# Layer 0 of a convolution stack: two-patch expansion rows first, then single-patch rows; convolution steps taken in pairs

## The chip, the core and the metric

The kernel runs on one core of a Trainium2 chip. The metric is the device time of one launch in microseconds, lower being better; the comparison uses medians of several launches of both kernels on the same chip.

## What is computed

The input `x` has four images of 64 channels, 256 x 256 pixels, in f32. Four layers follow, each of the form `x = x + layer(group_norm(x))`. The change touches the first layer alone, whose core in the reference is

```python
x = jnp.einsum('bchw,oc->bohw', x, w_in)            # 64 -> 384 channels
# per 8x8 patch: rfft2, times fft_filter, irfft2
x = lax.conv_general_dilated(x, w_dw, (1, 1), [(1, 1), (1, 1)], feature_group_count=C)   # 3x3 per channel
x1, x2 = jnp.split(x, 2, axis=1)
x = jax.nn.gelu(x1, approximate=False) * x2          # 192 channels
return jnp.einsum('bchw,oc->bohw', x, w_out)         # 192 -> 64 channels
```

Per channel, the patch filter and the 3 x 3 convolution are one linear map: the 64 outputs of an 8 x 8 patch depend on the 64 pixels of the patch itself and on those of its neighbours (right, below, diagonal, as the patches are cut here).

## The kernel before

Each image is an array of 32 x 32 patches. A **block** `p` is a strip of NR = 11 rows of patches in an image, and there are three to an image, so 12 blocks. A block is worked in four quarters `kb`, each of 48 hidden channels with their gate partners. A quarter has two stages:

1. **Expansion**, `expand(p, kb, t)`, for up to 12 rows `t` of patches. The normalized input `xn` of the row stands still in TensorE, and the weights `win` stream past. Even rows take two patches at a time (`pairs`, line 444: 32 instructions on tiles of 64 x 128), odd rows one patch at a time (line 450: 64 instructions on tiles of 64 x 64). The result lies in PSUM (`psu`) and is copied to the SBUF tile `u` by ScalarE (ACT) and VectorE (DVE), half a row each: four copies on each engine for a row of pairs (line 459), three for a row of singles (lines 461 to 463). Of the 12 blocks four have 12 rows and eight have 11, because a strip at the edge of the image lacks one.
2. **Convolution**, `convolve(p, kb, g)`, for 12 steps `g`. Each step first makes the patches' **own** products (line 494, tiles of 64 x 64, 16 instructions), then the **neighbours'** products, added to the same PSUM (line 503, 48 instructions, 64 rows by up to 28 columns). Then ACT applies GELU (line 510, twice) and DVE multiplies by the gate (line 511, twice); the result `h` is sent to DRAM by a DMA that GpSimd (POOL) issues (line 514).

Around the steps of block `p` stands other work, put there by hand:

- `unit()` runs one sixteenth of the last projection of block `p - 1`: `project` makes its products (lines 591 and 598) in a PSUM tile `po`, and DVE adds them to the residual `r` (line 607, or lines 610 and 612 and the statistics of line 618). `load_half` then issues the loads for a later unit on the queue of SyncE (SP).
- `load_w` loads weights of the convolution; `load_next` loads what the next block or image needs: in the first three quarters four-row pieces `st` of the next image, whose statistics `next_stats` takes on DVE (line 320, two instructions a piece), in the last quarter rows `x` of the next block, which `normalize_x` turns into `xn` on ACT (line 256). `next_norms` advances a waiting group norm by one of its parts.

The order on TensorE, DVE, ACT and SP is the order in which the program is written. PSUM is handed out by `banks` in strict rotation over four tiles of two banks: `tag=f"p{next(turn) % 4}"`. A row of expansion takes two of the four, a convolution step two, a unit one, so each use waits until the tile's previous content, four hand-outs back, has been copied or multiplied away.

The order of a quarter before:

```python
if t == NR - 2: load_w(...)
if t >= NR - 1: load_next(kb)
...
if g % 3 == 0: unit()
convolve(p, kb, g)
if g < 2: load_next(kb)
if g in (1, 2, 4, 5) and loaded: next_stats(b + 1, loaded.pop(0))
```

Of the kernel before, what the change touches and what calls it, by code (L numbers as in the profile page):

```python
# [18 lines left out]
HID = 192  # L19
# [102 lines left out]
class _Net:  # L122
# [152 lines left out]
    def _layer0(self, ctx, dst):  # L275
# [5 lines left out]
        def banks(name):  # L281

            return pp.tile([128, 2, 512], F32, tag=f"p{next(turn) % 4}", name=name)
# [11 lines left out]
        NR = 11  # L295
        L = CW * NR
        NG = PB // 4
# [134 lines left out]
        def expand(p, kb, t):  # L432

            b, i0 = blocks[p]
            ps = [banks(f"psu_{p}_{kb}_{t}_{s}") for s in range(2)]
            xn = xns[b, i0 + t]
            lo, hi = halves
            pairs = t % 2 == 0
            for k in range(2):
                for m in range(4):  # L440
                    n, at = 2 * (4 * k + m), slice(2 * PB * m, 2 * PB * (m + 1))
                    for s in range(2):
                        if pairs:
                            nc.tensor.matmul(  # L444
                                ps[s][:, k, at], xn[halves[s], n : n + 2].rearrange("p n r w -> p (n r w)"),
                                win[halves[s], kb, 0 : 2 * PB], start=True, stop=True,
                            )
                            continue
                        for odd in range(2):
                            nc.tensor.matmul(  # L450
                                ps[s][halves[1 - odd], k, at], xn[halves[s], n + odd].rearrange("p r w -> p (r w)"),
                                win[halves[s], kb, PB * (1 - odd) : PB * (3 - odd)], start=True, stop=True,
                            )
            at = lambda h, o: u[h, :, t * CW + o : t * CW + o + 8].rearrange("p c (s m) -> p c s m", s=2)
            for s, copy in enumerate((nc.scalar.copy, nc.vector.tensor_copy)):
                v = ps[s][:, :, 0 : 8 * PB].rearrange("p s (m c) -> p c s m", m=4)
                if pairs:
                    for h, o, k, c in ((lo, O1, lo, 0), (hi, O2, lo, PB), (lo, E1 + 1, hi, 0), (hi, E2 + 1, hi, PB)):
                        copy(at(h, 8 * s + o), v[k, c : c + PB])  # L459
                    continue  # L460
                copy(at(slice(0, 128), 8 * s + 1), v[:, 0:PB])
                copy(at(hi, 8 * s + E2 + 1), v[lo, PB:])
                copy(at(lo, 8 * s + O1), v[hi, PB:])  # L463
# [18 lines left out]
                tensor=v.tensor, offset=v.offset + down * CW + o, ap=[v.ap[0], [CW, NR], [step, 2], [1, HC]]  # L482
            )

        def convolve(p, kb, g):

            ps = [banks(f"pc_{p}_{kb}_{g}_{k}") for k in range(2)]
            G = NG * kb + g
            w = wl[p * (HID // 8) + G // 2]
            out = lambda lo, m, k, h: ps[k][lo : lo + m, h, 0:L].rearrange("p (i x j) -> p i x j", i=NR, x=2)  # L490
            for k in range(2):
                for c in range(2):
                    for h in range(2):
                        nc.tensor.matmul(  # L494
                            out(C * c, C, k, h), w[halves[h], k, 2 * (G % 2) + c, 0:C], cells(h, 4 * g + 2 * k + c, 0, 0),
                            start=True, stop=False, tile_position=(h * C, c * C), skip_group_check=True,
                        )
            for n, (c0, m, down, right) in enumerate(UNITS):
                for k in range(2):
                    for c in range(2):  # L500
                        q = C * c + Q * (1 - k)
                        for h in range(2):
                            nc.tensor.matmul(  # L503
                                out(q, m, k, h), w[halves[h], k, 2 * (G % 2) + c, c0 : c0 + m],
                                cells(h, 4 * g + 2 * k + c, down, right),
                                start=False, stop=(n == 2), tile_position=(h * C, q), skip_group_check=True,
                            )
            h = p_h.tile([128, 2, L], F32, tag="h", name=f"h_{p}_{kb}_{g}")
            for k in range(2):
                nc.scalar.activation(h[:, k], ps[k][:, 0, 0:L], AF.Gelu)  # L510
                nc.vector.tensor_mul(h[:, k], h[:, k], ps[k][:, 1, 0:L])  # L511
            if p not in gs:
                gs[p] = p_g.tile([2, HID // 2, 2 * Q, L], F32, tag="g", name=f"g_{p}")
            nc.gpsimd.dma_start(gs[p][:, 2 * G : 2 * G + 2].rearrange("k c p l -> (c p) k l"), h)  # L514

# [125 lines left out]
        with ordered:  # L641
# [44 lines left out]
            lo, hi = halves  # L686
# [6 lines left out]
            for p in range(NB + 1):  # L693
                units = iter([(r, half) for r in range(P) for half in range(2)] if p > 0 else [])
                ahead, first = 1, []
                if p == NB:
                    ctx_u.close()
                    sources.append([pool("l0g1e", 6), pool("l0g6e", 6), pool("l0re", 3)])
                    ahead = 3
                for r in range(ahead):  # L700
                    for half in range(2):
                        first.append((p - 1, r, half))
                        if p == NB:
                            load_half(*first.pop())

                def unit():
                    at = next(units, None)
                    if at:
                        project(p - 1, *at)
                        load_half(p - 1, at[0] + ahead, at[1])  # L710

                if p == NB:
                    for k in range(2 * P):
                        unit()
                    while self.norms:
                        self.next_norms()
                    break
                b, i0 = blocks[p]
                rows = rows_of(p)
                after = rows_of(p + 1) if p + 1 < NB else []  # L720
                fresh = [row for row in after if row not in xns]
                for t in (0, NR):
                    if not 0 <= i0 + t < NP:
                        nc.gpsimd.memset(rows_u[:, :, t], 0.0)
                nk = [] if b + 1 >= B else list(range(p % NI * NJ // NI, (p % NI + 1) * NJ // NI))
                loaded, begun = [], iter(fresh[:4])

                def load_next(kb):
                    if kb == 3:
                        row = next(begun, None)  # L730
                        if row:
                            load_x(row)
                    elif nk:
                        loaded.append(nk.pop(0))
                        load_stats(b + 1, loaded[-1])

                for kb in range(4):
                    for t in range(NR + 1):
                        if 0 <= i0 + t < NP:
                            expand(p, kb, t)  # L740
                        if t in (5, 8) and first:
                            load_half(*first.pop(0))
                        if t == NR - 2:
                            load_w(p * (HID // 8) + NG * kb // 2 + 3)
                        if t >= NR - 1:
                            load_next(kb)
                    for g in range(NG):
                        G = NG * kb + g
                        if g % 2 == 0 and g > 0:
                            load_w(p * (HID // 8) + G // 2 + 3)  # L750
                        if g % 3 == 0:
                            unit()
                        convolve(p, kb, g)
                        if g < 2:
                            load_next(kb)
                        if g < NG - 1:
                            self.next_norms()
                        if kb < 3:
                            if g in (1, 2, 4, 5) and loaded:
                                next_stats(b + 1, loaded.pop(0))  # L760
                        elif 0 <= g - 1 < len(fresh):
                            k = g - 1
                            normalize_x(fresh[k])
                            if k + 4 < len(fresh):
                                load_x(fresh[k + 4])
                for row in rows:
                    if row not in after:
                        xns.pop(row)
# [728 lines left out]
```

## Time and profile before

| | us |
|---|---|
| median of 3 launches (6493.61 to 6522.05) | 6502.17 |
| the profiled execution, own time | 6525.09 |
| its span, first to last instruction | 6523.3 |
| TensorE busy in it | 6001.2 (92%) |
| DVE busy | 4272.8 (66%) |
| ACT busy | 3240.4 (50%) |

The profile page gives, for one execution, the busy time of each engine, the chain of work that ended last, and groups of equal instructions by line with their count, busy time and mean duration, followed by the idle time of the engine just before them and what ended it. The timeline lists instructions in order of time, equal ones merged: start, length, engine, line. "PEld" is the loading of stationary weights in TensorE, shown beside "PE", the products. Layer 0 runs from about 101 us, where the first expansion starts, to about 3960 us.

### The profile page before, as it was taken

The numbers are of one execution on the slowest core, as the hardware profiler recorded it, in microseconds if no ns is written. First come the engines' busy times: TensorE is split into PE (matmuls) and PEld (weight loads), VectorE is DVE, ScalarE is ACT, GpSimd is POOL, SyncE is SP. The second block draws the span as 40 slices with busy tenths as digits, with TensorE's granted clock in tenths as the row PEclk, the third lists the DMA queues.
The fourth block names the chain that finished last, engine by engine and source line by source line (L and its number), as shares of the span: only waits on it lengthen the run. The fifth ranks groups of instructions, "written<-read, shape, count | busy, mean of one in ns | idle before, by whom it ended". The sixth has DMA issues, their size and how long they took to land.

```text
span 6523.3 us, 238228 instructions
## 1 busy us (share of the span) xinstructions
PE 6001.2 (92%) x106712; PEld 3199.7 (49%) x106712; DVE 4272.8 (66%) x5924; ACT 3240.4 (50%) x4564; POOL 1046.6 (16%) x1646
## 2 busy tenths in 40 slices
PE   2999999999999999999999977999899999999988
PEld 1455555555555555555555543333344444443566
DVE  5556665565655565655555546999798889885355
ACT  4344434344443444443444314777787778773211
POOL 3111111111111111111111111111122222221011
PEclk9999999999999999999999978999999999999855
DMA  8487879787888787886868779999576666667899
GB/s 242 136 218 214 230 207 232 218 242 219 245 220 243 219 236 206 229 223 199 228 195 226 207 198 244 226 229 228 148 180 174 170 173 181 170 176 268 325 353 398
DMA packets 878510, 1447.67 MB, mean 222 GB/s; under 512 B 77252, under 2 KB 586452, under 8 KB 875444
## 3 DMA queue, kind: packets, MB, share of 16 engines
q1 hardware_dynamic: 725284, 923.09, 55.9%
q0 software_dynamic: 148672, 500.14, 22.1%
q8 instruction: 843, 13.81, 0.9%
q10 hardware_dynamic: 3536, 9.20, 0.6%
q14 instruction: 175, 1.43, 0.1%
HBM read 932.08 MB, written 500.04 MB: 220 GB/s over the span
## 4 chain that ended last, share of the span: by engine, by line
PE 83%; DMA 7%; ACT 5%; issue 2%; DVE 2%; SPq 1%; POOL 0%; ACTq 0%; DVEq 0%; POOLq 0%
PE pc L503 18%; PE pc L494 12%; PE m L880 10%; PE psu L444 9%; PE one L1121 9%; PE div L1080 7%; ACT u L459 4%; PE psu L450 4%; PE po L591 4%; PE psz L1110 2%; DMA x<-x 2%; PE po L598 2%; DMA g<-g 2%; PE psa L1308 2%; DMA x<-in_x_dram 1%
## 5 line engine op out<-in xcount | busy, mean ns | idle before, releaser
L511 DVE TENSOR_TENSOR h<-h,pc 128x374 f32<-128x374 f32 x1152 | 575.3, 541 | 1216.7 <-ACT h L510 1216.5
L510 ACT ACTIVATE h<-pc 128x374 f32<-128x374 f32 x1152 | 493.1, 480 | 1762.0 <-PE pc L503 1745.9
L503 PE MATMUL pc<-u,w 64*16 64x374 f32 (+2 forms) x27648 | 1241.4, 480 | 3.0 <-issue 3.0
L514 POOL DMA_DIRECT2D g<-h x576 | 414.8, 720 | 2990.7 <-DVE h L511 2800.8
L494 PE MATMUL pc<-u,w 64*64 64x374 f32 x9216 | 881.2, 488 | 6.7 <-DVE u L463 3.9
L503 PEld LDWEIGHTS pc<-u,w 64*16 64x16 f32 (+2 forms) x27648 | 413.3, 92 | 763.5 <-issue 761.6
L444 PE MATMUL psu<-win,xn 64*128 64x96 f32 x8704 | 625.7, 283 | 137.2 <-ACT u L459 124.1
L459 DVE COPY u<-psu 64x384 f32<-64x384 f32 x1088 | 604.3, 555 | 155.1 <-PE psu L444 143.5
L444 PEld LDWEIGHTS psu<-win,xn 64*128 64x128 f32 x8704 | 574.8, 193 | 206.2 <-ACT u L459 159.9
L459 ACT COPY u<-psu 64x384 f32<-64x384 f32 x1088 | 560.5, 515 | 221.1 <-PE psu L444 201.0
L1066 DVE TENSOR_TENSOR q<-xn 128x2313 f32<-128x2313 f32 (+2 forms) x256 | 628.0, 2496 | 1.9 <-ACT xn L256 1.7
L1121 PE MATMUL one<-z,wp 32*32 32x512 f32 x16384 | 598.0, 599 | 19.0 <-issue 14.9
L256 ACT ACTIVATE xn<-x,nb,r 128x1024 f32<-128x1024 f32 (+3 forms) x272 | 486.7, 1792 | 212.4 <-DMA x<-x 140.5
L494 PEld LDWEIGHTS pc<-u,w 64*64 64x64 f32 x9216 | 332.2, 132 | 451.1 <-issue 359.7
L1067 ACT ACTIVATE q<-q 128x2313 f32<-128x2313 f32 (+2 forms) x256 | 529.0, 2087 | 30.8 <-DVE q L1066 29.3
L450 PE MATMUL psu<-win,xn 64*64 64x96 f32 x17408 | 456.5, 253 | 79.3 <-issue 48.6
L1080 PE MATMUL div<-q,ones 64*32 64x512 f32 x8192 | 471.1, 602 | 13.8 <-ACT q L1067 10.9
L1121 PEld LDWEIGHTS one<-z,wp 32*32 32x32 f32 x16384 | 367.2, 103 | 229.7 <-issue 88.3
L450 PEld LDWEIGHTS psu<-win,xn 64*64 64x64 f32 x17408 | 396.8, 138 | 121.4 <-issue 66.7
L1154 POOL DMA_DIRECT2D x<-r x512 | 273.9, 544 | 977.8 <-DVE r L1151 963.9
L591 PE MATMUL po<-g,wo 128*64 128x176 f32 (+1 forms) x3072 | 314.9, 348 | 74.3 <-DMA g<-g 37.9
L880 PE MATMUL m<-t,wk 64*64 64x512 f32 x3072 | 341.1, 588 | 0.0
(162 smaller groups left out, 6672.9 us busy)
## 6 DMA issues: line engine op xcount, KB each, us to landing
g<-h POOLq DMA_DIRECT2D x576, 374.0 KB, 6.4
x<-x SPq DMA_DIRECT2D x240, 640.0 KB, 6.4
w<-wt SPq DMA_DIRECT2D x288, 448.0 KB, 7.0
x<-x SPq DMA_DIRECT2D x100, 1024.0 KB, 14.2
g<-g SPq DMA_DIRECT2D x414, 187.0 KB, 5.0
g<-g SPq DMA_DIRECT2D x736, 93.5 KB, 5.3
x<-in_x_dram SPq DMA_DIRECT2D x256, 256.0 KB, 8.2
x<-o POOLq DMA_DIRECT2D x128, 512.0 KB, 8.2
```

The source lines that it names most:

```text
L444: nc.tensor.matmul(ps[s][:, k, at], xn[halves[s], n : n + 2].rearrange("p n r w -> p (n r w)"), win[halves[s], kb, 0 : 2 * PB], start=True ...
L450: nc.tensor.matmul(ps[s][halves[1 - odd], k, at], xn[halves[s], n + odd].rearrange("p r w -> p (r w)"), win[halves[s], kb, PB * (1 - odd) ...
L459: copy(at(h, 8 * s + o), v[k, c : c + PB])
L494: nc.tensor.matmul(out(C * c, C, k, h), w[halves[h], k, 2 * (G % 2) + c, 0:C], cells(h, 4 * g + 2 * k + c, 0, 0), start=True, stop=False, ...
L503: nc.tensor.matmul(out(q, m, k, h), w[halves[h], k, 2 * (G % 2) + c, c0 : c0 + m], cells(h, 4 * g + 2 * k + c, down, right), start=False, ...
L511: nc.vector.tensor_mul(h[:, k], h[:, k], ps[k][:, 1, 0:L])
L591: nc.tensor.matmul(out(k, s, x), wo1, moving(g1[:, 2 * k], 2 * half + k, s, x), start=(x == 0), stop=False, skip_group_check=True,)
L880: nc.tensor.matmul(rows2(m)[halves[j], s], w[dx][halves[s]], ts[n][halves[s], i, 2 * j : 2 * j + 2, dx : dx + W], start=(dx == 0), stop=(d ...
L1066: nc.vector.tensor_sub(d, p0, p1)
L1067: nc.scalar.activation(d, d, AF.Square)
L1080: ins = nc.tensor.matmul(ps[quarters[j], h], ones[halves[h]], q[n, g, k][halves[h], r + 2 * j : r + 2 * j + 2, o : o + W], start=(m == 0), ...
L1121: ins = nc.tensor.matmul(rows2(ps[g])[quarters[j], k], w[quarters[i]], z[quarters[i], h, 2 * j + dy : 2 * j + dy + 2, dx : dx + W], tile_p ...
```

## The change

The expansion makes the same number of rows of each kind, but in another order: `pairs` holds for `t < 6` instead of even `t`. `convolve` is split at its middle into `own` and `beside`, and the steps are taken two at a time: `own(g)`, `own(g + 1)`, `beside(g)`, `beside(g + 1)`. With it the surrounding work moves: units come before steps 0, 2, 6 and 8 instead of 0, 3, 6 and 9; the weights of the first load and one `load_next` come at the last row of the expansion, and the others before pairs 0, 2 and 4 (in the last quarter two rows at each of two calls); statistics come at the end of each pair while pieces wait; `normalize_x` runs for two rows at the end of a pair; `next_norms` is called after five of six pairs instead of after eleven of twelve steps.

```diff
-            pairs = t % 2 == 0
+            pairs = t < (NR + 1) // 2
...
-        def convolve(p, kb, g):
+        pcs = {}
+        def own(p, kb, g):
-            ps = [banks(f"pc_{p}_{kb}_{g}_{k}") for k in range(2)]
+            ps = pcs[g] = [banks(f"pc_{p}_{kb}_{g}_{k}") for k in range(2)]
...
+        def beside(p, kb, g):
+            ps = pcs.pop(g)
...
                     if kb == 3:
-                        row = next(begun, None)
-                        if row:
+                        for _, row in zip(range(2), begun):
                             load_x(row)
...
-                        if t == NR - 2:
+                        if t == NR:
                             load_w(p * (HID // 8) + NG * kb // 2 + 3)
-                        if t >= NR - 1:
                             load_next(kb)
-                    for g in range(NG):
-                        G = NG * kb + g
-                        if g % 2 == 0 and g > 0:
-                            load_w(p * (HID // 8) + G // 2 + 3)
-                        if g % 3 == 0:
+                    for g in range(0, NG, 2):
+                        if g > 0:
+                            load_w(p * (HID // 8) + (NG * kb + g) // 2 + 3)
+                        if g in (0, 2, 6, 8):
                             unit()
-                        convolve(p, kb, g)
-                        if g < 2:
+                        if g < 6:
                             load_next(kb)
-                        if g < NG - 1:
+                        for k in range(2):
+                            own(p, kb, g + k)
+                        for k in range(2):
+                            beside(p, kb, g + k)
+                        if g < NG - 2:
                             self.next_norms()
                         if kb < 3:
-                            if g in (1, 2, 4, 5) and loaded:
+                            if loaded:
                                 next_stats(b + 1, loaded.pop(0))
-                        elif 0 <= g - 1 < len(fresh):
-                            k = g - 1
+                            continue
+                        for k in range(g, min(g + 2, len(fresh))):
                             normalize_x(fresh[k])
                             if k + 4 < len(fresh):
                                 load_x(fresh[k + 4])
```

More of the change, by code (lines that the diff above doesn't have):

```diff
@@ L497, in convolve @@
                         )
+        def beside(p, kb, g):
+            ps = pcs.pop(g)
+            G = NG * kb + g
+            w = wl[p * (HID // 8) + G // 2]
+            out = lambda lo, m, k, h: ps[k][lo : lo + m, h, 0:L].rearrange("p (i x j) -> p i x j", i=NR, x=2)
             for n, (c0, m, down, right) in enumerate(UNITS):
```

## The prediction

> **What bounds the kernel now.** I read the page's chain first: where does the time that sets the end lie?
>
> ```profile
> PE 83%; DMA 7%; ACT 5%; issue 2%; DVE 2%; SPq 1%; POOL 0%; ACTq 0%; DVEq 0%; POOLq 0%
> PE pc L503 18%; PE pc L494 12%; PE m L880 10%; PE psu L444 9%; PE one L1121 9%; PE div L1080 7%; ACT u L459 4%; PE psu L450 4%; PE po L591 4%; PE psz L1110 2%; DMA x<-x 2%; PE po L598 2%; DMA g<-g 2%; PE psa L1308 2%; DMA x<-in_x_dram 1%
> ```
>
> TensorE carries it. In the convolution (L494, L503) it does so alone; in the expansion (L444, L450) 4% of the span runs through ACT's copies, L459. So the two stages have different limits and I read each from its timeline.
>
> Convolution: the timeline of weight loads through one step and into the next. A group of products starts with its weights, so these starts are a clock (start, length, line).
>
> ```profile
> 1402.91 0.21 PEld L494 LDWEIGHTS pc<-u,w 64*64 64x64 f32 x8 [0.66 <-issue]
> 1403.28 0.16 PEld L494 LDWEIGHTS pc<-u,w 64*64 64x64 f32 x4 [0.16 <-issue]
> 1403.59 0.17 PEld L494 LDWEIGHTS pc<-u,w 64*64 64x64 f32 x4 [0.15 <-issue]
> 1404.36 0.15 PEld L503 LDWEIGHTS pc<-u,w 64*16 64x16 f32 x16 [0.60 <-issue]
> ...
> 1405.65 0.13 PEld L503 LDWEIGHTS pc<-u,w 64*4 64x4 f32 x8 [0.19 <-issue]
> 1406.43 0.21 PEld L494 LDWEIGHTS pc<-u,w 64*64 64x64 f32 x8 [0.65 <-issue]
> ```
>
> Groups inside a half follow each other by 0.31 us. The loads at 1403.59 run one group ahead, so two groups lie between them and the first L503: 0.77 = 0.31 + 0.46. The same at the other end, 1405.65 to 1406.43: 0.31 + 0.47. Each change of half costs 0.15 or 0.16 us, and the first group after it in L494 another 0.06 (0.37, not 0.31). The PE timeline of a step behind a projection shows what a missing change is worth:
>
> ```profile
> 1386.13 0.85 PE L598 MATMUL po<-g,wo 64*64 64x160 f32 x16
> 1386.81 1.46 PE L494 MATMUL pc<-u,w 64*64 64x374 f32 x16
> 1388.20 2.14 PE L503 MATMUL pc<-u,w 64*16 64x374 f32 x48
> 1390.27 1.53 PE L494 MATMUL pc<-u,w 64*64 64x374 f32 x16
> 1391.72 2.14 PE L503 MATMUL pc<-u,w 64*16 64x374 f32 x48
> ```
>
> From start to next start, own products take 1.39 us behind L598, which has the same 64 x 64 tiles, and 1.45 behind neighbours' products; the latter take 2.07.
>
> Expansion: the DVE timeline of alternating rows, then who waited for whom between 432 and 3780 us (total, times, longest).
>
> ```profile
> 1359.62 2.26 DVE L459 COPY u<-psu 64x384 f32<-64x384 f32 x4 [0.45 <-PE psu L444]
> 1361.91 0.56 DVE L461 COPY u<-psu 128x384 f32<-128x384 f32 x1
> 1362.49 0.55 DVE L462 COPY u<-psu 64x384 f32<-64x384 f32 x1
> 1363.05 0.56 DVE L463 COPY u<-psu 64x384 f32<-64x384 f32 x1
> 1364.06 2.26 DVE L459 COPY u<-psu 64x384 f32<-64x384 f32 x4 [0.45 <-PE psu L444]
> ```
>
> ```profile
> PE psu L444 <- ACT u L459: 114.1, 170, 1.6
> ```
>
> DVE works 3.99 of each 4.44 us and then waits 0.45 for TensorE, which itself waits some 0.6 us for PSUM before each row of pairs. Neither engine is full: a slow copy (pairs) must end before a slow product (the next pairs) can start, with only a short single row between.
>
> **What the Trainium skill says.** "TensorEngine Tiling (Array Packing)", Key Properties: changing the tiling mode, not just the tile, drains TensorE. The trace agrees: 0.15 us at 64 x 64 to narrow columns and back, nothing at L598 to L494. The same page, PSUM Bottleneck: packed products may leave the PSUM copies as the limit, to be shared by ScalarE and VectorE. It agrees in the rows: DVE 3.99 of 4.44 us. "TensorE: Matmul & The Clock Gate", What's actually happening: the clock halves after idle windows of some 3.4 us. The stretches of layer 0 show 0.98 to 1.00 granted, so I book no clock gain.
>
> **The change, part by part.**
>
> *Conv pairs.* A quarter (four for each of 12 blocks, so 48) has 12 own-to-neighbour changes; six remain, each 0.15. Changes straight back to own products, without a unit or the expansion between: 11 - 3 = 8 before, 5 - 3 = 2 after; each 0.16 + 0.06. So 6 x 0.15 + 6 x 0.22 = 2.22 us a quarter, x 48 = **-106 us**. The first block has no units, but the same difference: 11 to 5. No instruction is added; own(g + 1) behind own(g) should run at 0.31 a group, as L494 does behind L598.
>
> *Rows.* Six (five) rows of pairs follow each other. DVE needs 2.28 for one (4 x 0.56 and gaps). The loop over two PSUM halves needs, from the copies of a row to those of the row two later, 2.37 (release 1361.69 on PE to copies 1364.06) + 2.26, so 2.31 a row: about equal, DVE nearly full. Single rows: DVE 1.70, loop (1.7 + 1.7)/2, the same. A pair of rows costs 4.02 instead of 4.44. A stage's filling and emptying remain, so some 5.5 such pairs count for 12 rows, 4.5 for 11: 16 x (5.5 + 4.5 + 4.5) x 0.42 = **-97 us**. The end of the copies after TensorE's last row stays as far behind (both orders end in single rows, or the unit covers it).
>
> *New wait, po.* At pair g the rotation gives po the oldest tile, and own(g + 1)'s second half needs it back. Before, a whole step (3.5 us) lay between; now only own(g). With T the end of the previous neighbours' products: the multiplies L511 end at T + 1.63 (1406.43 against 1407.06 + 1.00). If statistics follow (two L320 of 0.68) DVE reaches the additions at T + 3.0 and ends them at T + 4.45 (L607, 1.41 to 1.45) or 4.6 (L610 and L612, 0.8 each). TensorE wants the tile at T + 2.07 (unit) + 1.25 + 0.63 = T + 3.95. So it stalls about 0.5 us, and both neighbours' halves queue behind. Pieces wait at the end of pairs 0, 2, 4, 6 and units stand before 2, 6, 8: three cases in a quarter with four pieces, 7 or 8 a block, 23 an image, three images, less 7 for the block without units: 62 x 0.5 = **+31 us**. Without statistics the additions start when the products are there, T + 2.15, and end by T + 3.8: no stall.
>
> *Loads, norms.* Nothing is added on SP or POOL. load_w moves two rows later, still ahead of its use at step 6 by 20 us against a median landing of 7.0. SP meets load_x for rows 2 and 3 behind the dozen issues of the unit's load_half, some 9 us into the stage, and ACT wants them at about 18: landing takes 8.2 at the median, and ACT already waited 22.4 us for x between 800 and 2000. A late row blocks the GELUs behind normalize_x; TensorE has two to three us of other work. A late st piece blocks DVE at L320 likewise. I take **+10 us**, 0 to 60. POOL's h issues (0.72) come in twos, 2 us apart, with 4 buffers and 14 us to the reuse: no cost; were that cover gone, each GELU would wait for a landing of 6.4. The norm's third part, three times in all, may delay ACT by 2 us: nothing.
>
> Sum: -106 - 97 + 31 + 10 = **-162 us**, against the profiled execution's own 6525.09 (span 6523.3), so 6363 there. That execution lies 23 us above the median of the runs shown, 6502.17; I give the time on the median's scale: 6502 - 162 = **6340 us**.
>
> **Bounds of what the trace doesn't show.** Own behind own: at best no gap (taken), at worst half the change cost stays (+50). Pairs behind pairs: DVE bound alone, 3.98, gives -107; if the loop took 2.45, -60. The po stall: 0 to 1.5 each, 0 to +93.
>
> **The rivals.**
>
> *A, PSUM handed back too late (faster, but less).* In a pair without unit, own(g + 3) starts 1.31 us after the last neighbours' products of g + 1 and needs a tile whose multiply ends 1.18 after them: a margin of 0.1. If ACT or DVE runs 0.4 late, each of the 5 x 48 hand-overs stalls: 96 us, so 6436. For it: the margin. Against: the view shows ACT and DVE idle 2 us and more before each step's GELU.
>
> *B, in-order queues blocked by late loads (slower).* If x and st pieces land more than some 12 us after issue, ACT (last quarter) or DVE (first three) stands, and the GELUs of two steps queue behind instead of one. It decides when each of the 11 blocks that fetch ahead loses over 17.7 us (195/11), giving over 6535; at 22 us, 6580. For: DMA engines are busy 0.83 of the time and will have 5% less. Against: only 22.4 us of such waits in four blocks, mostly beside TensorE's work.
>
> *C, nothing moves.* The changes of half or row might only shift the wait: 6500. The built program does have the new order on TensorE, so no effect would mean that DVE or DMA was the true bound; the idle times above speak against it.
>
> **How the numbers follow.** 0.5% (33 us) is about what a measurement of this kernel can tell from no change. Forecast 0.66, A 0.18 (also faster), B 0.08, C 0.08. Faster 0.84, same 0.08, slower 0.08. The forecast alone spans 6285 (full gains, no stall) to 6400; to leave out no more than 2 in 10 the range takes in A: 6285 to 6445.
>
> **What would show it.** Right: the L444 row's wait for ACT falls from 124 to under 40 us on the page; DVE copies run without the 0.45 gaps; a pair of steps takes 6.7 us, not 7.05; quarters are 49 us or less in the convolution (50.5 to 53 now) and 22 to 24 in the expansion (24 to 27). Stalls of own products on L607 or L612 near 0.5 us, some 62 times, show the new wait. Wrong: gaps between own(g) and own(g + 1) of 0.15, or waits on L511 before every pair, or DMA st and x ending long waits of DVE and ACT.

## The result, and the profile after

The changed kernel takes **6426.33 us** (median of 4, 6421.78 to 6442.22) against 6498.26 for the kernel before on the same chip; ratio 0.9874, 95% interval 0.9845 to 0.9902. That is 72 us less between these medians, and 82 by the ratio. The forecast was 162 less: right in sign, within its range, about twice too large. The two profiled executions lie 103 us apart (spans 6523.3 and 6420.0), because that of before is slower than any of the four runs shown. So the stages below, which are read from these two, sum to 13 to 23 us more than the runs gained, and in which term is not known.

The page's chain of the changed kernel:

```profile
PE 79%; DVE 8%; DMA 6%; ACT 3%; issue 3%; SPq 1%; ACTq 0%; POOL 0%; DVEq 0%; POOLq 0%
PE pc L512 17%; PE pc L496 11%; PE m L889 10%; PE one L1130 9%; PE div L1089 7%; PE psu L444 5%; DVE u L459 5%; PE psu L450 4%; PE po L600 4%; PE psz L1119 2%; PE po L607 2%; PE psa L1317 2%; PE psy L1464 2%; ACT u L459 2%; DMA g<-g 2%
```

DVE rose from 2% to 8%: the expansion now runs through its copies, as intended. The DVE timeline of one expansion, quarter 1 of a block with 12 rows (start, length, instructions merged):

```profile
1386.28 13.75 DVE L459 COPY u<-psu 64x384 f32<-64x384 f32 x24 [0.46 <-PE psu L444]
1400.06 0.56 DVE L461 COPY u<-psu 128x384 f32<-128x384 f32 x1
1400.64 0.55 DVE L462 COPY u<-psu 64x384 f32<-64x384 f32 x1
1401.20 0.56 DVE L463 COPY u<-psu 64x384 f32<-64x384 f32 x1
1401.79 0.56 DVE L461 COPY u<-psu 128x384 f32<-128x384 f32 x1
```

Six rows of pairs are 24 copies in 13.75 us, 2.29 a row, without the gaps of 0.45; a single row takes 1.73. Who waited for whom on TensorE in layer 0:

```profile
PE psu L450 <- issue: 57.2, 47, 5.5
PE psu L444 <- ACT u L459: 51.5, 48, 20.7
```

The wait of pair rows for ACT fell from 124.1 (186 times) to 51.5. The prediction's sign was under 40; a single wait of 20.7 in the first block stands in this sum, where before it had fallen on a single row (21.7, counted under L450), so the rest is 31. But a line that the prediction had not read is now on top. Before it was

```profile
PE psu L450 <- issue: 48.6, 35, 3.4
```

that is, TensorE standing in single rows for nothing that the profile shows (the view calls this "issue"). The PE timeline of a pair behind a unit:

```profile
1342.43 0.85 PE L607 MATMUL po<-g,wo 64*64 64x160 f32 x16
1343.11 2.11 PE L496 MATMUL pc<-u,w 64*64 64x374 f32 x24
1345.50 0.88 PE L496 MATMUL pc<-u,w 64*64 64x374 f32 x8 [0.29 <-DVE r L621]
1346.31 4.06 PE L512 MATMUL pc<-u,w 64*16 64x374 f32 x96
```

Three quarters of the own products run, then the last eight wait for po. The DVE timeline of the same moment says why:

```profile
1341.36 1.00 DVE L520 TENSOR_TENSOR h<-h,pc 128x374 f32<-128x374 f32 x2 [0.93 <-ACT h L519]
...
1342.79 1.28 DVE L320 BATCH_NORM_STATS2 bst<-st 128x6 f32<-128x512 f32 x2
1343.99 0.73 DVE L619 TENSOR_TENSOR r<-r,po 128x320 f32<-128x320 f32 x1
1344.62 0.73 DVE L621 TENSOR_TENSOR r<-r,po 128x320 f32<-128x320 f32 x1
```

The statistics stand ahead of the additions, which end at 1345.35. So the new wait is there, at its place.

Where did the time go? I cut TensorE's timeline into its 48 expansions and 48 convolution stages (from the first product of one to the first of the next, where the products of a unit ahead of step 0 belong to the convolution; the last convolution includes the end of the layer) and subtracted the profiled executions:

| us, after less before | quarter 0 | 1 | 2 | 3 | sum |
|---|---|---|---|---|---|
| expansion | +26.3 | -30.4 | -23.3 | -17.8 | -45.2 |
| convolution | -13.9 | -9.4 | -18.4 | -7.7 | -49.4 |

Quarters 1 to 3 of the expansion gave -71.5, 2.0 us a stage, the number that was forecast (97/48). Quarter 0 went the other way. The convolution gave -49 where -75 was due (-106 and +31).

### The profile page after: what moved, and what is told of

The parts are those of the page before. It is cut to its first block, busy times and chain, and to the rows that moved or that the text cites. A ratio compares the mean times of both kernels' runs of the same rounds, so it can differ in the third digit from the quotient of the medians.

```text
span 6420.0 us, 238128 instructions
## 1 busy us (share of the span) xinstructions
PE 5955.1 (93%) x106712; PEld 3302.7 (51%) x106712; DVE 4271.0 (67%) x5924; ACT 3242.5 (51%) x4564; POOL 1048.4 (16%) x1646
## 3 DMA queue, kind: packets, MB, share of 16 engines
q1 hardware_dynamic: 725284, 923.09, 55.7%
## 4 chain that ended last, share of the span: by engine, by line
PE 79%; DVE 8%; DMA 6%; ACT 3%; issue 3%; SPq 1%; ACTq 0%; POOL 0%; DVEq 0%; POOLq 0%
PE pc L512 17%; PE pc L496 11%; PE m L889 10%; PE one L1130 9%; PE div L1089 7%; PE psu L444 5%; DVE u L459 5%; PE psu L450 4%; PE po L600 4%; PE psz L1119 2%; PE po L607 2%; PE psa L1317 2%; PE psy L1464 2%; ACT u L459 2%; DMA g<-g 2%
## 5 line engine op out<-in xcount | busy, mean ns | idle before, releaser
L520 DVE TENSOR_TENSOR h<-h,pc 128x374 f32<-128x374 f32 x1152 | 575.2, 542 | 1178.0 <-ACT h L519 1177.9
L512 PE MATMUL pc<-u,w 64*16 64x374 f32 (+2 forms) x27648 | 1178.6, 479 | 6.0 <-issue 6.0
L496 PE MATMUL pc<-u,w 64*64 64x374 f32 x9216 | 831.6, 485 | 13.8 <-DVE u L463 4.6
L512 PEld LDWEIGHTS pc<-u,w 64*16 64x16 f32 (+2 forms) x27648 | 465.7, 92 | 683.1 <-issue 645.0
L444 PE MATMUL psu<-win,xn 64*128 64x96 f32 x8704 | 596.0, 282 | 72.8 <-ACT u L459 51.5
L450 PE MATMUL psu<-win,xn 64*64 64x96 f32 x17408 | 491.7, 251 | 93.7 <-issue 57.2
L496 PEld LDWEIGHTS pc<-u,w 64*64 64x64 f32 x9216 | 359.7, 132 | 391.9 <-issue 164.4
L450 PEld LDWEIGHTS psu<-win,xn 64*64 64x64 f32 x17408 | 426.5, 136 | 154.1 <-issue 82.3
```

The source lines that it names most:

```text
L444: nc.tensor.matmul(ps[s][:, k, at], xn[halves[s], n : n + 2].rearrange("p n r w -> p (n r w)"), win[halves[s], kb, 0 : 2 * PB], start=True ...
L450: nc.tensor.matmul(ps[s][halves[1 - odd], k, at], xn[halves[s], n + odd].rearrange("p r w -> p (r w)"), win[halves[s], kb, PB * (1 - odd) ...
L496: nc.tensor.matmul(out(C * c, C, k, h), w[halves[h], k, 2 * (G % 2) + c, 0:C], cells(h, 4 * g + 2 * k + c, 0, 0), start=True, stop=False, ...
L512: nc.tensor.matmul(out(q, m, k, h), w[halves[h], k, 2 * (G % 2) + c, c0 : c0 + m], cells(h, 4 * g + 2 * k + c, down, right), start=False, ...
```

## The experiments

All kernels are compared with the kernel before by ratio, with the 95% interval.

**One half of the change at a time: rows alone (e1).** The kernel before with

```diff
-            pairs = t % 2 == 0
+            pairs = t < (NR + 1) // 2
```

> The kernel before with the one-line change of the row order alone (rows of pairs first). In the changed kernel 36 of 48 expansion stages, those of quarters 1 to 3, became 2.0 us shorter each, as forecast, but the stages of quarter 0 together 26 us longer instead of 24 shorter. Theory (the loss of quarter 0 comes from rows x that land late after the paired steps, not from the row order): all 48 stages gain some 2 us, -80 to -97, so about 6410 against 6498. Rival (the row order itself runs into the late rows, since a denser start of a quarter wants them earlier): quarter 0 stays as it was or worse, -70 or less, 6430 to 6450.

Measured: 6462.48 us, ratio 0.9938 (0.9921 to 0.9955), about -40. By stages: quarter 0 +30.1, the others -28.4, -21.4 and -30.9; the convolution -3. So quarter 0 is lost with the rows alone, while ACT's waits for x are no longer than before (29.9 us against 35.5). My theory of late rows falls. What did grow is the issue wait of single rows in quarter 0, summed over its gaps in the timeline: 45.8 us against 12.6; in quarters 1 to 3 it fell instead, to 16 in all from 36.

**Pairs alone (e2).** The changed kernel with `pairs = t % 2 == 0`.

> The changed kernel with the rows of the expansion alternating again as before. Theory: the paired products give 0.30 us a pair, 288 pairs, -86; the wait for po takes back 20 to 30; late rows of x take back some 40 to 50 in quarter 0. Sum -10 to -25: 6475 to 6490. Rival (the pairs give all that was forecast, and the loss sits in the expansion): -75 or more, 6425 or less.

Measured: 6493.79 us, ratio 0.9985 (0.9974 to 0.9995), about -10. The convolution gave -52.5, as in the changed kernel; the expansion lost 32, in all four quarters (9, 4, 7 and 12), not in quarter 0 alone. The number came, its cause did not: issue waits of the rows are 21 us longer than before (76.3 against 55.7, both kinds of row), late x in quarter 0 is not what took it. Why the old row order meets more of these waits when the convolution is shorter stays open.

**Loads of x ahead of those of g, last quarter (e3).** In the changed kernel

```diff
                         project(p - 1, *at)
-                        load_half(p - 1, at[0] + ahead, at[1])
+                        if p < NB and kb == 3:
+                            held.append((p - 1, at[0] + ahead, at[1]))
+                        else:
+                            load_half(p - 1, at[0] + ahead, at[1])
...
                             if k + 4 < len(fresh):
                                 load_x(fresh[k + 4])
+                        while held:
+                            load_half(*held.pop(0))
```

> The changed kernel; in the last quarter alone, the loads of g (load_half) of a unit are issued behind the loads of x at the end of the pair instead of at once, so that the rows x no longer queue behind a dozen issues on SP. Theory (rows 6 and 7 are issued 7 us late because SP is at the g loads, and what is late stays late to the end of the quarter): ACT's waits for x fall from 83 to under 40 us, the expansion of quarter 0 shortens by 2 to 4 us in each of 11 blocks, -25 to -45, 6380 to 6400. Rival (ACT is late because it normalizes two rows at a time, or because DMA bandwidth is short): no change, 6415 to 6435.

Measured: 6509.67 us, ratio 1.0011 (0.9999 to 1.0023), 83 us slower than the changed kernel. Waits on TensorE in layer 0:

```profile
PE po L600 <- DMA g<-g: 83.9, 20, 8.8
```

The mechanism came, the gain did not. ACT's waits for x fell from 75.1 to 4.7 us, and quarter 0's expansion went from +26.3 to +1.4; but the units of the last quarter now wait for their g, 4.2 us at a time, and its convolution grew by 90 us. In this queue a load that goes first makes another one late.

**Statistics behind the unit (e4).** In the changed kernel

```diff
+                        if g > 0 and kb < 3 and loaded:
+                            next_stats(b + 1, loaded.pop(0))
                         for k in range(2):
                             own(p, kb, g + k)
...
                         if kb < 3:
-                            if loaded:
-                                next_stats(b + 1, loaded.pop(0))
                             continue
```

> The changed kernel with the statistics of a waiting piece (two bn_stats on DVE) taken behind the unit's additions at the start of the next pair instead of ahead of them at the end of the pair. Theory (the second own product waits for po, because DVE takes the statistics first): the 62 stalls of 0.3 to 0.5 us go, -20 to -30, 6396 to 6406, and the own halves behind a unit take 2.7 us with no tail of 3.0. Rival (the stalls were hidden or are of another kind): within 8 us of the changed kernel.

Measured: 6396.15 us, ratio 0.9846 (0.9823 to 0.9869). That is 30 below the changed kernel by medians and 18 by the ratios, whose intervals overlap, so the total alone doesn't part the two. The stages do: those of the convolution went from -49.4 to -75.0. The PE timeline of a pair behind a unit has no gap any more:

```profile
1340.65 0.85 PE L607 MATMUL po<-g,wo 64*64 64x160 f32 x16
1341.32 2.76 PE L496 MATMUL pc<-u,w 64*64 64x374 f32 x32
```

So the wait for po cost 26 us by stages. (The view of waits showed only 3.2 us for it: a product is drawn 0.47 us long while its successor starts 0.31 after it, so a stall must exceed the difference to be seen.)

**The old order of products, all else as changed (e7).**

```diff
                         for k in range(2):
                             own(p, kb, g + k)
-                        for k in range(2):
                             beside(p, kb, g + k)
```

> The changed kernel with the products of a pair in the old order (own, neighbours', own, neighbours'), all else as changed: rows, units, loads, statistics. Theory: the halves change twice as often, 0.30 us a pair, 288 pairs, +86; the wait for po goes with it (a whole step lies between again), -20 to -30: 6480 to 6495 against 6426. Rival (the gain of the convolution came from moving units and loads, not from the order of the products): 6440 or less.

Measured: 6454.51 us, ratio 0.9928 (0.9913 to 0.9943), 28 above the changed kernel, between the two expectations. The convolution stages stand at -2.8, so moving units and loads gave nothing; against the -75.0 of e4, which like this one has no wait for po, the order of products is worth **72 us** by stages, not 106. The whole kernels lie 58 us apart by medians and 53 by ratios: the expansion is 7 us shorter in e7, and the profiled execution of e4 is the fastest of its five, 13 below their median. So 72 is rather the upper end.

**A new theory for quarter 0.** The Trainium skill's page "Runtime: NRT & Kernel Launch", Instruction fetch mechanics, says that an engine's instructions come by DMA in blocks of 16 KiB, 256 instructions, while it runs, and that this is mostly hidden. The traces have an instruction queue with packets of 16 KB. A single row is 64 products and 64 weight loads, 128 instructions in 1.7 us; two such rows use up a block. A row of pairs is 64 instructions in 2.3 us. In quarter 0 the loads for the first unit, which must wait until the block's g is written, go out just then. So singles in a run need instructions fastest while DMA is full. The PE timeline of quarter 0 in block 2, in e4:

```profile
706.06 1.91 PE L450 MATMUL psu<-win,xn 64*64 64x96 f32 x64
708.22 2.05 PE L450 MATMUL psu<-win,xn 64*64 64x96 f32 x65 [0.25 <-ACT u L459]
712.11 2.95 PE L450 MATMUL psu<-win,xn 64*64 64x96 f32 x126 [1.85 <-issue]
720.37 3.08 PE L450 MATMUL psu<-win,xn 64*64 64x96 f32 x65 [5.31 <-issue]
```

The trace's instruction packets start at 697.6, 709.2, 717.8 and 721.6: TensorE goes on 2.9 and 2.6 us after the two in the middle.

The trace doesn't say whose packets these are, but their number does. The profile page of the changed kernel:

```profile
PE 5955.1 (93%) x106712; PEld 3302.7 (51%) x106712; DVE 4271.0 (67%) x5924; ACT 3242.5 (51%) x4564; POOL 1048.4 (16%) x1646
...
q8 instruction: 843, 13.81, 0.9%
```

At the skill page's 256 instructions each, an estimate, 843 packets hold 215,808 instructions. TensorE's records in that trace, products, weight loads and its sequencer's own, are 215,775. And the waits end where the packets do: in the changed kernel the rows' products have 36 waits of over 0.4 us for nothing shown, and all 36 end 1.2 to 1.8 us after the end of such a packet (in the kernel before all 38, in e4 all 41). Of the 62 waits of that length with a shown cause 15% end so.

The stretches of this quarter's singles and of quarter 1's in the same block (PE, PEld, DVE, ACT and POOL busy, clock, DMA share, GB/s):

```profile
704.00:722.00 18.00, 10.41 (x325) 9.34 (x328) 10.72 (x20) 9.99 (x20) 0.00 (x0) 0.96 0.83 177
...
785.00:796.00 11.00, 9.86 (x344) 8.87 (x342) 9.80 (x18) 8.86 (x19) 0.00 (x0) 1.00 0.02 5
```

The same run of singles takes 18 us with DMA busy 0.83 of the time and 11 us at 0.02. Three kernels, all edits of e4, test this.

**Alternating rows in quarter 0 alone (e8).**

```diff
-            pairs = t < (NR + 1) // 2
+            pairs = t % 2 == 0 if kb == 0 else t < (NR + 1) // 2
```

> The kernel of e4_stats_behind_unit (6396) with the old alternating row order in quarter 0 alone. New theory: in quarter 0 the run of single rows, 128 TensorE instructions in 1.7 us, waits for its instructions, whose fetches come late among the burst of g and x loads (issue stalls of single rows in quarter 0: 39 us, 13 before); alternation spreads the need. The stalls fall back to 10 to 17 us, the expansion of quarter 0 is 15 to 30 us shorter in all, 6366 to 6385. Rival (late rows of x make quarter 0 long, whatever the order): within 8 us of 6396 or slower by the 20 that DVE's fullness gave.

Measured: 6379.68 us, ratio 0.9818 (0.9801 to 0.9835). Issue waits of singles in quarter 0 fall from 38.6 to 16.2 us and its expansion from +21.8 to +9.0. As the theory says. This is the lowest median of the versions that do the whole work, though its interval overlaps with those of e4 and e10.

**Singles first in quarter 0 (e10).**

```diff
+            pairs = (t >= (NR + 1) // 2) if kb == 0 else t < (NR + 1) // 2
```

> The kernel of e4_stats_behind_unit with single rows first and rows of pairs last in quarter 0 alone (the edge blocks then have one row of pairs more or less in that quarter). DMA is busy from the start of quarter 0 (0.99 in its first 14 us of the one looked at, 0.77 in the rest). Theory (instruction need times DMA load): singles at the start meet the same or a denser load, stalls stay at 25 to 45 us, 6385 to 6405. Rival (only the loads of g for the first unit, some 9 us into the stage, are to blame): stalls below 15, 6365 to 6380.

Measured: 6386.17 us, ratio 0.9831 (0.9811 to 0.9851); issue waits of singles in quarter 0 41.3 us. They stay where the theory has them: a run of singles stalls at either end of this quarter. Yet its expansion stands at +11.4, 10 us below e4 and nearly as short as in e8, where the stalls had fallen by 22 us. So the gain of e8 can't be put down to the stalls alone; what else shortens this quarter stays open. The time is 10 us below e4, which the intervals don't part.

**Without the loads (e11).** The tiles g of the first two units of each block but the last are set to zero instead of loaded, so this kernel leaves out a part of the work.

```diff
+            if blank:   # r == 0 and p < NB - 1
+                nc.gpsimd.memset(g1, 0.0)
+                nc.gpsimd.memset(g6, 0.0)
+                return
             q0 = 4 * half
             for x, p0, q, n in planes(r):
```

> The kernel of e4_stats_behind_unit, in which the g tiles of the first two units of each block but the last are set to zero by GpSimd instead of loaded from DRAM: some 24 loads less in quarter 0. Its output is not the reference's in those rows. Theory (the DMA burst delays TensorE's instruction fetches): issue stalls of single rows in quarter 0 fall from 39 to under 15 us, 6360 to 6378. Rival (fetching is too slow for six single rows in a row, with or without other DMA): stalls stay above 30 us, 6385 or more.

Measured: 6366.02 us, ratio 0.9797 (0.978 to 0.9813). The PE timeline and the stretch of the same singles as above:

```profile
700.96 4.22 PE L450 MATMUL psu<-win,xn 64*64 64x96 f32 x132
705.35 3.43 PE L450 MATMUL psu<-win,xn 64*64 64x96 f32 x125 [0.18 <-DVE u L463]
709.40 1.66 PE L450 MATMUL psu<-win,xn 64*64 64x96 f32 x63 [0.62 <-issue]
```

```profile
700.00:711.00 11.00, 10.05 (x339) 8.74 (x337) 10.06 (x19) 8.94 (x18) 0.00 (x0) 1.00 0.07 16
```

Issue waits of singles in quarter 0 are 4.4 us, and its expansion stands at **-20.4** instead of +21.8. The forecast's share for it was -24. ACT's waits for x are as long as before the edit (77.4 us, 74.9 in e4), so it is not late rows that went away. Six singles in a row are not too fast for the fetch; they are too fast for the fetch beside this burst. The instruction packets themselves take 1.1 to 1.3 us in e4's stretch and 0.9 to 1.4 here; what the burst changes is when they start, 8.6 us apart at the worst in e4's run of singles and some 4 here. TensorE had stood for 2.7 us when that late one started. Why it started late is not shown.

**All loads, but later (e12).** From e4, to have that gain in a kernel that loads everything:

```diff
-                        if t in (5, 8) and first:
-                            load_half(*first.pop(0))
...
-                        if g in (0, 2, 6, 8):
+                        if g in ((6, 8, 10), (0, 2, 4, 6, 8), (0, 2, 6, 8), (0, 2, 6, 8))[kb]:
                             unit()
+                        if g in (2, 4) and first:
+                            load_half(*first.pop(0))
```

> The kernel of e4_stats_behind_unit, in which the loads of a block's first two units are issued on SP before pairs 2 and 4 of quarter 0, behind a weight load that waits for the first pair, and so behind the expansion; the units run before steps 6, 8, 10 of quarter 0, then 0, 2, 4, 6, 8 of quarter 1. All loads are made. Theory (the burst of loads in the expansion of quarter 0 delays instruction fetches): stalls of single rows in quarter 0 below 15 us (39 in e4), the expansion of quarter 0 some 35 to 40 us shorter in all, as without the loads, 6355 to 6375 against 6396. Rival (the burst costs as much wherever it stands, since instructions are fetched in the convolution too, or the units now wait for g): 6385 to 6410.

Measured: 6500.58 us, ratio 1.0003 (0.999 to 1.0017), far outside both. Against e4 the expansion of quarter 0 is 36 us shorter, as the theory had it, and everything is given back at once: the convolutions of quarters 0 and 1 are 85 and 35 us longer (one unit has moved from the first to the second). Waits on TensorE in layer 0:

```profile
PE po L600 <- DMA g<-g: 79.6, 35, 11.3
...
PE pc L496 <- DVE u L463: 19.7, 17, 2.0
```

Units wait for g, and own products for the last copies of the expansion, which a unit used to cover.

## Why the forecast came out twice too large

| term | forecast | measured, us by stages | from |
|---|---|---|---|
| order of products | -106 | -72 | e4 against e7 |
| rows, quarters 1 to 3 | -73 | -71.5 | after against before |
| rows, quarter 0 | -24 | +26.3 (-20.4 without the burst) | after against before; e11 against before |
| wait for po | +31 | +26 | after against e4 |
| late x and st | +10 (0 to 60) | not separable | |

The first four measured terms make -91; the stages of the profiled executions differ by -94.6, and the runs by 72 to 82.

- **Rows.** The mechanism holds, and its size per row: 2.29 us a pair row on DVE (2.31 forecast), 1.73 a single (1.70). The step that failed is the factor 16 x (5.5 + 4.5 + 4.5), which took all quarters as alike. In quarter 0 a run of singles meets the burst of loads, and TensorE waits for its instructions: 39 us in the changed kernel, 13 before. The hint was in the view of waits: 48.6 us of issue in L450, 35 times. In quarters 1 to 3 the agreement of -71.5 with -73 is partly luck. The shortest stages without such a wait went from 26.4 to 24.4 us with 12 rows, and from 23.6 and 24.2 to 22.1 and 22.6 with 11 rows: 2.0, 1.5 and 1.6 us, which makes 61 in 36 stages. The waits of these quarters' rows for instructions fell too, from 42.5 to 19.6 us, which the forecast did not have; other waits took a part back.
- **Products.** The mechanism holds: own(g + 1) follows own(g) at 0.31 us a group, with no gap. The term was mis-sized. An undisturbed pair takes 2.75 + 4.00 = 6.75 us (6.7 forecast) against 7.05 before: 0.30, not 0.37. In the weight-load starts of e4 the changes that remain cost 0.47 to 0.51 where 0.46 was taken, and groups of neighbours' products run at 0.31 to 0.33. That explains some 20 of the 34 us; most of the rest lies in the last quarter, whose convolution gave only 10.5 of -75.0 in e4. I did not take that apart.
- **The wait for po.** Right in place, cause and, by stages, in size, from the order of DVE's queue and the rotation of PSUM alone.
- **Loads.** ACT's waits for x doubled, from 35.5 to 75.1 us, by the queueing behind load_half that the prediction described: in e3, where those loads go second, they are 4.7. They are 47.5 in e7, which has the changed kernel's loads and the old order of products, so the denser products add to them. In e3 their removal went with 25 us less in quarter 0's expansion, but g moved as well, so that is no price for them alone.
- **The rivals.** A's waits on L511 (now L520) before every pair did not appear: 6.3 us in six waits, and those at the first rows of an expansion. B has a part of the truth in another form: loads did get in the way, not by landing late but by holding up TensorE's instructions. C did not come: the interval ends at 0.9902.
- **The clock.** The prediction's 0.98 to 1.00 leaves out the end of layer 0, where 0.70 was granted (3780 to 3960 us; 0.74 in the changed kernel's last 186 us). All expansions and all but the last of the convolution stages lie ahead of it, so no term rests on it.

## What to carry to other kernels

Group work of one tile shape on TensorE, and rows of equal copy time, and count each change of shape from the weight-load starts. But ask of each stage what DMA does meanwhile, since a change that makes instructions denser needs them fetched in time. Before moving a load, list what stands behind it in its queue: here x ahead of g and g later each brought their gain and returned all of it. When two uses of a rotating PSUM tile come closer together, look at what stands ahead of its release in the in-order queue of the engine that frees it, and put that work behind.

## What the hardware showed that I had not expected

TensorE stood up to 5.5 us in the changed kernel for nothing but its next instructions. In e4 it stood 5.3 us in a stretch with a DMA share of 0.83; with that share at 0.02 (quarter 1) or 0.07 (e11) the same rows had one such stall, of 0.6 us. The Trainium skill's sentence ("Runtime: NRT & Kernel Launch", Instruction fetch mechanics) that the fetch is mostly hidden holds for quarters 1 to 3 of the changed kernel (19.6 us of such waits in the rows of 36 stages), and not for quarter 0 (39 us in 12). That the packets seen are TensorE's own is read from their number and from where the waits end; the trace doesn't name their engine.
